# Layer 2's gate matmuls turned round: gate weights stationary in four column groups of TensorE

## The chip, the core and the metric

The kernel runs on one core of one Trainium2 chip. The metric is the device time of one execution in microseconds (us). The core has a matrix engine (TensorE, PE in the profile, with its weight loads shown as PEld), a vector engine (DVE), a scalar engine (ACT), GpSimd (POOL) and a queue engine that issues DMAs (SP). Each has its own queue of instructions and takes them in order.

## What is computed

Four graph layers follow each other on `x` [16, 1024, 128] with one adjacency matrix `adj` [16, 1024, 1024] of zeros and ones; after each of them stands a residual and a layer norm. The change lies in layer 2, whose gates are three columns per node:

```python
# layer 2 (L2_gnn); F = 128, ig_w, fg_w, og_w are [1, 256]
h = x @ W_w.T + W_b
e = (h @ A) @ h.T;  e = e + swap(e)
att = softmax(where(adj > 0, e, 0), axis=1) * adj
h_prime = relu(att @ h)
concat = concatenate([x, h_prime], axis=-1)          # [.., 256]
i_c = sigmoid(concat @ ig_w.T + ig_b)                # one number a node
f_c = sigmoid(concat @ fg_w.T + fg_b)
o_c = sigmoid(concat @ og_w.T + og_b)
h_joint = sigmoid(i_c * h_prime + f_c * x)
return o_c * tanh(h_joint)
# x = layernorm(x + layer 2);  layer 3 (two graph convolutions) follows
```

## The kernel before

The work is in three stretches: layer 0 with the loading of `adj` (up to about 750 us of the span), layer 1 with its sequential thinning of the adjacency (to about 1900 us), and layers 2 and 3 together (about 1930 us to the end, 3075 us). The change touches the last stretch.

There the 16 batches go through three generators, which `in_turn` lets take turns: for each `b`, `attention(b)` runs beside `after(b - 1)` and `before(b + 1)`. `before` makes layer 1's output (products of `hb` with `Wl`, turned into `yn`), adds it to `xn`, norms it (`normed`) and makes `xT`, `hT`, `G`, `hn`. `attention` has eight tiles of 128 nodes: two score matmuls (`pmm`, line 723), a masked maximum on DVE (`em`, L1564), an Exp on ACT (L1568), a scale by the sum (`hs`, L1575) and two matmuls into `acc` (L1578). `after` makes `hpT`, the relu of `acc` (L1584), the gates (L1585 to L1593), the gated sum `yn` (L1596 to L1603), a norm, and then layer 3: eight casts of the adjacency to `A` (four on ACT, L1614, four on DVE, L1627), `x3T` (L1618), a product with `U0` and two elu (L1490 to L1492 and L1486 to L1488), a product with `U1` (L1501) whose result is split into `zhi` and `zlo`, a propagation by `A` (L1515, 32 matmuls), the same again with `U2`, and the sum and its norm.

The gates before are 16 small matmuls a batch. For each tile `i` of 128 nodes, the nodes are the stationary operand and the three gate vectors stream past them:

```python
pg = ps_h.tile([P, NT, 3], F32, name="pg", tag="h")
for i in range(NT):
    c = slice(i * P, (i + 1) * P)
    nc.tensor.matmul(pg[:, i, :], s.xT[:, c], gw[:, 0, :], start=True, stop=False)
    nc.tensor.matmul(pg[:, i, :], hpT[:, c], gw[:, 1, :], start=False, stop=True)
```

The result `pg` has nodes on partitions, which is what the gating needs. It lives in the PSUM pool `ps_h`, which has two buffers, shared by every turned tile and every product of `before` and `after`. A float32 matmul with a full stationary operand shows as two weight loads and two matmul records in the trace; a transpose by `identf` shows as one of each.

`normed` takes eight BatchNorm statistics on DVE (L777, L779), a power on GpSimd (L744), a small product on DVE (`ln_nb`, L782) and eight ACT instructions on `xn` (L784).

The order of the instructions in each engine's queue is not that of the text: a scheduler sets it when the kernel is built, from its own estimate of durations and from which buffers are free. The generators only give it the sequence of the program.

Of the kernel before, what the change touches and what calls it, by code (L numbers as in the profile page):

```python
# [9 lines left out]
F32 = mybir.dt.float32  # L10
# [12 lines left out]
P = 128  # L23
# [616 lines left out]
def fast_kernel(ctx: ExitStack, tc: tile.TileContext, t: dict, out: bass.AP, flag: bass.AP):  # L640

    nc = tc.nc
    B, N, D = t["x"].shape
    NT = N // P
# [6 lines left out]
    identf = consts.tile([P, P], F32, name="identf")  # L651
# [34 lines left out]
    def nat(ap):  # L686
        return ap.rearrange("(t p) d -> p t d", p=P)

    def row_bcast(pool, src, n, name, bufs=1):

        v = pool.tile([P, n], F32, name=name, bufs=bufs)
        nc.sync.dma_start(v, bass.AP(tensor=src.tensor, offset=src.offset, ap=[[0, P], [1, n]]))
        return v

    def column(pool, src, name):
        v = pool.tile([P, 1], F32, name=name)
        nc.sync.dma_start(v, bass.AP(tensor=src.tensor, offset=src.offset, ap=[[1, P], [1, 1]]))
        return v

    def matrix(pool, src, name, bufs=1):  # L700
        v = pool.tile([P, P], F32, name=name, bufs=bufs)
        nc.sync.dma_start(v, src)
        return v

    def transposed(pool, psum, src, name, tag="tr"):
        v = pool.tile([P, P], F32, name=name)
        p = psum.tile([P, P], F32, name="wtr", tag=tag)
        nc.tensor.transpose(p, src, identf)
        nc.vector.tensor_copy(v, p)
        return v  # L710
# [16 lines left out]
    def tiles3(ap):  # L727
        return ap.rearrange("p (t d) -> p t d", d=P)

    def per_row(v):  # L730

        return v[:, :, None].to_broadcast([P, NT, P])
# [28 lines left out]
    def products(psum, *pairs):  # L761

        for p, c, _ in halves(psum):
            for i, (W, x) in enumerate(pairs):
                nc.tensor.matmul(p, W, x[:, c], start=(i == 0), stop=(i == len(pairs) - 1))  # L765
            yield p, c

    def half_rows(v):

        return v[:, :, None].to_broadcast([P, 4, P])  # L770
# [42 lines left out]
    def symmetric(pool, psum, A, name, tag="tr"):  # L813
        As = pool.tile([P, P], F32, name=name)
        p = psum.tile([P, P], F32, name="wtr", tag=tag)
        nc.tensor.transpose(p, A, identf)
        nc.vector.tensor_add(As, A, p)
        return As
# [49 lines left out]
    with ExitStack() as ph:  # L868

        early = ph.enter_context(tc.tile_pool(name="l0_early", bufs=1, reuse_waits="tile"))  # L870
        wts = ph.enter_context(tc.tile_pool(name="l0_w", bufs=1, reuse_waits="tile"))
        ps_w = ph.enter_context(tc.tile_pool(name="l0_pw", bufs=2, space=PSUM, reuse_waits="tile"))
        ps_a = ph.enter_context(tc.tile_pool(name="l0_pa", bufs=1, space=PSUM, reuse_waits="tile"))
        ps_h = ph.enter_context(tc.tile_pool(name="l0_ph", bufs=2, space=PSUM, reuse_waits="tile"))
# [7 lines left out]
        gw = wts.tile([P, 2], F32, name="l0gw")  # L882
        with nc.allow_non_contiguous_dma(reason="a vector of 256"):
            nc.sync.dma_start(gw, t["L0_gnn_gate_w"].rearrange("o (h d) -> d (o h)", d=P))
        gb = row_bcast(wts, t["L0_gnn_gate_b"], 1, "l0gb")
# [285 lines left out]
    class Layers23:  # L1171
# [8 lines left out]
        def weights(self, ps_h):  # L1180
            wts = self.wts
            self.Wl = wts.tile([P, 3, P], F32, name="Wl")
            nc.sync.dma_start(self.Wl, nat(t["L1_gnn_Wl"]))
            self.blcol = column(wts, t["L1_gnn_bl"], "blcol")
            self.W2T = transposed(wts, ps_h, matrix(wts, t["L2_gnn_W_w"], "l2W"), "l2WT", "h")
            self.b2 = column(wts, t["L2_gnn_W_b"], "l2b")
            self.As2 = symmetric(wts, ps_h, matrix(wts, t["L2_gnn_A"], "l2A"), "l2As", "h")
            self.gw = wts.tile([P, 2, 3], F32, name="l2gw")
            self.gb = wts.tile([P, 3], F32, name="l2gb")
            for i, n in enumerate(("ig", "fg", "og")):  # L1190
                with nc.allow_non_contiguous_dma(reason="a vector of 256"):
                    nc.sync.dma_start(self.gw[:, :, i], t[f"L2_gnn_{n}_w"].rearrange("o (h d) -> d (o h)", d=P))
                src = t[f"L2_gnn_{n}_b"]
                nc.sync.dma_start(self.gb[:, i:i + 1], bass.AP(tensor=src.tensor, offset=src.offset, ap=[[0, P], [1, 1]]))
            self.U = [matrix(wts, t[f"L3_gnn_W{i}"], f"U{i}") for i in range(3)]
            self.c = [column(wts, t[f"L3_gnn_b{i}"], f"c{i}") for i in range(3)]
            self.nbig = wts.tile([P, 1], F32, name="nbig")
            nc.vector.memset(self.nbig, -BIG)
# [26 lines left out]
    with ExitStack() as ph:  # L1225
        wts = ph.enter_context(tc.tile_pool(name="l1_w", bufs=1, reuse_waits="tile"))
# [5 lines left out]
        ps_h = ph.enter_context(tc.tile_pool(name="l1_ph", bufs=4, space=PSUM, reuse_waits="tile"))  # L1232
# [232 lines left out]
    with ExitStack() as ph:  # L1465
# [4 lines left out]
        ps_h = ph.enter_context(tc.tile_pool(name="l2_ph", bufs=2, space=PSUM, reuse_waits="tile"))  # L1470

        W2T, b2, As2, gw, gb, nbig, blcol, Wl = l2.W2T, l2.b2, l2.As2, l2.gw, l2.gb, l2.nbig, l2.blcol, l2.Wl
# [3 lines left out]
        def wide(name, bufs=1, dtype=F32):  # L1476
            return work.tile([P, N], dtype, name=name, bufs=bufs)

        def rows(name, bufs=1, dtype=F32):
            return work.tile([P, NT, P], dtype, name=name, bufs=bufs)  # L1480
# [100 lines left out]
        def after(s, b):  # L1581

            hpT = wide("hpT")
            nc.scalar.activation(hpT, s.acc, AF.Relu)  # L1584
            pg = ps_h.tile([P, NT, 3], F32, name="pg", tag="h")  # L1585
            for i in range(NT):
                c = slice(i * P, (i + 1) * P)
                nc.tensor.matmul(pg[:, i, :], s.xT[:, c], gw[:, 0, :], start=True, stop=False)
                nc.tensor.matmul(pg[:, i, :], hpT[:, c], gw[:, 1, :], start=False, stop=True)
            gt = small.tile([P, NT, 3], F32, name="gt")  # L1590
            nc.vector.tensor_add(gt, pg, gb[:, None, :].to_broadcast([P, NT, 3]))
            nc.scalar.activation(gt, gt, AF.Tanh, scale=0.5)
            nc.vector.tensor_scalar(gt, gt, 0.5, 0.5, op0=OP.mult, op1=OP.add)  # L1593
            yn = rows("yn", 2)
            for p, c, k in turned(ps_h, hpT):
                nc.vector.tensor_mul(yn[:, k, :], tiles3(p), half_rows(gt[:, k, 0]))  # L1596
            f = rows("x3T")
            nc.vector.tensor_mul(f, s.xn, per_row(gt[:, :, 1]))
            nc.vector.tensor_add(yn, yn, f)
            nc.scalar.activation(yn, yn, AF.Tanh, scale=0.5)  # L1600
            nc.scalar.activation(yn, yn, AF.Tanh, scale=0.5, bias=half)
            nc.vector.tensor_mul(yn, yn, per_row(gt[:, :, 2]))
            nc.vector.tensor_add(s.xn, s.xn, yn)  # L1603
            yield
            normed(small, s.xn)
            diag = bass.AP(tensor=s.A8.tensor, offset=s.A8.offset, ap=[list(s.A8.ap[0]), [N + P, NT], [1, P]])
            nc.vector.tensor_tensor(diag, diag, identb[:, None, :].to_broadcast([P, NT, P]), op=OP.add, saturate=False)
            dB = wide("dB")
            nc.sync.dma_start(dB, bass.AP(tensor=dinv_d.tensor, offset=dinv_d.offset + b * N, ap=[[0, P], [1, N]]))
            yield  # L1610

            A = work.tile([P, NT, N], F32R, name="A")
            for jt in range(NT // 2):
                nc.scalar.copy(A[:, jt, :], s.A8[:, jt, :])  # L1614
            db = dinv[:, b * NT:(b + 1) * NT]
            x3T = wide("x3T")
            for p, c, _ in turned(ps_h, s.xn):
                nc.scalar.copy(x3T[:, c], p)  # L1618
            h0 = wide("ehi", 2)
            for p, c in products(ps_h, (U0, x3T)):  # L1620
                elu(h0[:, c], p, c0)
            h1 = wide("ehi", 2)
            for h in range(H2):
                c = slice(h * 512, (h + 1) * 512)
                elu(h1[:, c], h0[:, c], None)
            for jt in range(NT // 2, NT):
                nc.vector.tensor_copy(A[:, jt, :], s.A8[:, jt, :])  # L1627
            yield
            parts = scaled_parts(h1, U1, db)
            yield  # L1630
            r = propagated(parts, A, dB)
            h2 = wide("ehi", 2)
            for h in range(H2):
                c = slice(h * 512, (h + 1) * 512)
                elu(h2[:, c], r[:, c], c1)
            yield
            parts = scaled_parts(h2, U2, db)
            yield
            r = propagated(parts, A, dB)
            nc.scalar.activation(r, r, AF.Identity, bias=c2)  # L1640
            yield
            for p, c, k in turned(ps_h, r):
                nc.vector.tensor_add(s.xn[:, k, :], s.xn[:, k, :], tiles3(p))
            normed(small, s.xn)
            nc.gpsimd.dma_start(nat(out[b]), s.xn)
            yield
# [49 lines left out]
```

## Time and profile before

| what | value |
|---|---|
| median of 15 runs | 3075.3 us (3066.54 to 3083.15) |
| the profiled execution | 3077.22 us, its span 3075.4 us |
| mean granted TensorE clock in it | 0.965 |
| PE / DVE / ACT / POOL busy | 93% / 76% / 66% / 10% |
| the chain that ended last, by engine | PE 61%, issue 17%, DVE 13%, ACT 4% |
| `pg` matmul records | 512, the first at 1934.6 us, the last at 3000.6 us |

The busy shares are over the whole span, and matmuls are pipelined, so that PE's busy time counts each record from its start to its modelled end. The granted clock is the share of TensorE's full speed that the throttle let through; the profile gives it for any stretch. Times within the span are read as us from its start; a period below is the time from the first gate matmul of one batch to that of the next.

### The profile page before, as it was taken

What the parts mean: (1) busy time and instruction counts of PE and PEld (TensorE: products, weight loads), DVE (VectorE), ACT (ScalarE), POOL (GpSimd) and SP (SyncE); (2) the same over time, 40 slices, a digit from 0 to 9 for tenths busy, and PEclk for the clock granted to TensorE, in tenths of its full rate; (3) what the DMA queues carried; (4) which work ended last, traced back from release to release, by engine and by line L of the source; (5) the groups of instructions that cost most, each with busy time, mean ns of one, the idle gap of its engine ahead of it and who ended that gap; (6) DMA issues with size and microseconds to landing.
All of it is one profiled execution on the core that took longest, in us unless ns stands there. A gap on an engine that the chain in (4) does not pass through costs nothing.

```text
span 3075.4 us, 43116 instructions
## 1 busy us (share of the span) xinstructions
PE 2856.3 (93%) x15379; PEld 1838.2 (60%) x15442; DVE 2327.9 (76%) x5971; ACT 2015.2 (66%) x3393; POOL 314.7 (10%) x292
## 2 busy tenths in 40 slices
PE   7999999997899999999999987999999999999995
PEld 4454555444566566777788874556555555555554
DVE  8788888886899996666688785766767676767765
ACT  6777777775678877565555534766666666667753
POOL 0000000003000001111122231000000000000000
PEclk9999999998999999999999998999999999999997
DMA  5344334441000014223367693111121221111000
GB/s 187 124 137 151 130 131 151 136 133 40 2 2 2 2 79 161 83 93 121 124 214 238 241 329 109 35 55 55 62 69 55 63 76 60 55 55 55 21 14 22
DMA packets 123216, 297.98 MB, mean 97 GB/s; under 512 B 12656, under 2 KB 64624, under 8 KB 115824
## 3 DMA queue, kind: packets, MB, share of 16 engines
q1 hardware_dynamic: 102384, 211.13, 20.7%
q0 software_dynamic: 20608, 84.00, 7.4%
q8 instruction: 124, 2.03, 0.3%
q14 instruction: 100, 0.82, 0.1%
HBM read 211.04 MB, written 84.02 MB: 96 GB/s over the span
## 4 chain that ended last, share of the span: by engine, by line
PE 61%; issue 17%; DVE 13%; ACT 4%; POOL 3%; DMA 2%; SPq 0%; POOLq 0%; DVEq 0%; ACTq 0%
PE pmm L723 10%; PE acc L1272 10%; PE ph L1515 7%; PE ph L765 6%; PE acc L1578 6%; PE acc L956 5%; PE ph L758 4%; PE ph L1376 4%; PE ph L1501 2%; POOL ln_rstd L744 2%; PE acc L1249 2%; ACT xn L784 2%; DVE ln_st L777 2%; DMA an<-in_adj 1%; DVE carry L908 1%
## 5 line engine op out<-in xcount | busy, mean ns | idle before, releaser
L723 PE MATMUL pmm<-G,hT 128*128 128x512 f32 x1024 | 522.1, 627 | 17.2 <-DVE mx L945 14.7
L723 PEld LDWEIGHTS pmm<-G,hT 128*128 128x128 f32 x1024 | 182.3, 198 | 182.4 <-issue 114.1
L1578 PE MATMUL acc<-em,hs 128*128 128x512 f32 x512 | 257.1, 614 | 12.1 <-DVE hs L1575 10.5
L956 PE MATMUL acc<-em,hs 128*128 128x512 f32 x512 | 240.5, 606 | 24.6 <-DVE hs L953 23.3
L784 ACT ACTIVATE xn<-xn,ln_nb,ln_rstd 128x128 f32<-128x128 f32 x512 | 206.5, 481 | 80.5 <-DVE ln_nb L782 80.4
L1272 PE MATMUL acc<-a,lo 128*128 128x512 f32 x768 | 241.1, 398 | 2.0 <-DVE lo L1240 2.0
L1272 PE MATMUL acc<-a,hi 128*128 128x512 f32 x768 | 241.8, 399 | 1.1 <-ACT hi L1239 0.9
L744 POOL TENSOR_TENSOR ln_rstd<-ln_rstd,mhalf 128x8 f32<-128x8 f32 x64 | 105.4, 1647 | 1297.6 <-DVE ln_rstd L741 1226.9
L1121 ACT ACTIVATE q<-s,negc 128x512 f16<-128x512 f32 x256 | 170.5, 697 | 59.4 <-DVE negc L1100 22.3
L1119 PE MATMUL s<-step,carry 128*128 128x384 bf16 (+3 forms) x1034 | 199.1, 303 | 7.9 <-DVE carry L1089 3.2
L1564 DVE CUSTOM_DVE_ANT_0 em<-pmm,msk 128x1024 f32<-128x1024 f32 x128 | 156.0, 1219 | 53.2 <-PE pmm L723 50.6
L1133 ACT ACTIVATE carry<-pc,negone 128x512 fp8e4<-128x512 f32 x256 | 166.8, 699 | 38.2 <-PE pc L1132 29.0
L900 ACT ACTIVATE ab<-an 128x1024 bf16<-128x1024 f32 x128 | 134.6, 1052 | 73.8 <-PE pt L907 36.5
L903 DVE SCALAR_TENSOR_TENSOR chk<-an 128x1024 fp8e4<-128x1024 f32 x128 | 156.2, 1220 | 35.0 <-DMA an<-in_adj 34.4
L956 PEld LDWEIGHTS acc<-em,hs 128*128 128x128 f32 x512 | 93.7, 191 | 143.1 <-issue 105.9
L1559 ACT ACTIVATE msk<-A,nbig 128x1024 bf16<-128x1024 fp8e4 x128 | 146.0, 1141 | 49.5 <-DVE mx L1564 47.6
L942 ACT ACTIVATE msk<-carry,l0nbig 128x1024 bf16<-128x1024 fp8e4 x128 | 145.4, 1140 | 44.5 <-DVE mx L945 40.4
L908 DVE TENSOR_SCALAR carry<-pt 128x1024 fp8e4<-128x1024 bf16 x128 | 155.8, 1219 | 23.4 <-PE pt L907 23.4
L1272 PEld LDWEIGHTS acc<-a,lo 128*128 128x128 f32 x768 | 142.8, 188 | 42.9 <-DVE lo L1240 9.5
L1272 PEld LDWEIGHTS acc<-a,hi 128*128 128x128 f32 x768 | 141.6, 188 | 34.0 <-ACT hi L1239 1.4
L945 DVE CUSTOM_DVE_ANT_0 em<-pmm,msk 128x1024 f32<-128x1024 f32 x128 | 155.4, 1214 | 6.9 <-PE acc L956 4.8
L949 ACT ACTIVATE em<-em,nmx 128x1024 f32<-128x1024 f32 x128 | 145.9, 1140 | 20.8 <-DVE nmx L947 17.3
(278 smaller groups left out, 6524.9 us busy)
## 6 DMA issues: line engine op xcount, KB each, us to landing
an<-in_adj SPq DMA_DIRECT2D x128, 512.0 KB, 3.3
adj_d<-carry POOLq DMA_DIRECT2D x16, 1024.0 KB, 4.9
A<-dil_d SPq DMA_DIRECT2D x16, 1024.0 KB, 6.7
rdeg<-rdeg_d SPq DMA_DIRECT2D x32, 512.0 KB, 4.2
ag_d<-ag POOLq DMA_DIRECT2D x32, 512.0 KB, 5.3
ag<-ag_d SPq DMA_DIRECT2D x32, 512.0 KB, 6.2
A<-adj_d SPq DMA_DIRECT2D x16, 1024.0 KB, 4.8
xn<-in_x SPq DMA_DIRECT2D x16, 512.0 KB, 3.9
```

Of the source, the lines that this page charges most:

```text
L723: nc.tensor.matmul(p[:, h * 512:(h + 1) * 512], lhsT, rhs[:, h * 512:(h + 1) * 512], start=True, stop=True)
L744: nc.gpsimd.tensor_tensor(r, r, mhalf[:, :n], op=OP.pow)
L765: nc.tensor.matmul(p, W, x[:, c], start=(i == 0), stop=(i == len(pairs) - 1))
L784: nc.scalar.activation(r[:, i, :], r[:, i, :], AF.Identity, scale=rstd[:, i:i + 1], bias=nb[:, i:i + 1])
L908: nc.vector.tensor_scalar(Y[b][:, :, it * P:(it + 1) * P], pt, 0.0, None, op0=OP.is_gt, saturate=False)
L956: nc.tensor.matmul(s.acc[:, c], hs, em[:, c], start=(jt == 0), stop=(jt == NT - 1))
L1119: nc.tensor.matmul(s[:, lo or 0:], y, twos if lo is None else step[:, :512 - lo], start=(j == 0), stop=(j == len(terms) - 1))
L1121: nc.scalar.activation(q[:, h * 512:(h + 1) * 512], s, AF.Abs, bias=st.negc[:, i:i + 1])
L1133: nc.scalar.activation(Y[b][:, hb, ks], pc, AF.Relu, bias=negone, saturate=False)
L1272: nc.tensor.matmul(acc, part[:, jt, :], pieces[h * NT // 2 + i][:, j, :], start=(jt == 0 and p == 0), stop=(jt == NT - 1 and p == 1))
L1515: nc.tensor.matmul(p, part[:, jt, :], A[:, jt, c], start=(jt == 0 and i == 0), stop=(jt == NT - 1 and i == 1))
L1578: nc.tensor.matmul(s.acc[:, c], hs, em[:, c], start=(jt == 0), stop=(jt == NT - 1))
```

## The change

The gate weights become the stationary operand, padded with zeros to 32 columns, and the nodes stream past them. The 1024 nodes are cut into four quarters of 256; each quarter goes to a column group of 32 columns of TensorE and lands on 32 partitions of one PSUM tile `pq`. The result has gates on partitions, so ACT copies it to SBUF (into the tile of `x3T`, which is free then) and two transposes bring nodes to partitions again. Beside that, the gate weights are zeroed once by DVE before their three DMAs fill in the real columns.

```diff
+    def gates(psum, out, *pairs):
+        p = psum.tile([P, N // 4], F32, name="pq", tag="h")
+        for i, (g, x) in enumerate(pairs):
+            for q in range(4):
+                nc.tensor.matmul(p[32 * q:32 * q + 32, :], g, x[:, q * N // 4:(q + 1) * N // 4], start=(i == 0),
+                                 stop=(i == len(pairs) - 1), tile_position=(0, 32 * q))
+        nc.scalar.copy(out, p)
+        p = psum.tile([P, 2, P], F32, name="pg", tag="h")
+        for t in range(2):
+            nc.tensor.transpose(p[:, t, :], out[:, t * P:(t + 1) * P], identf)
+        return p.rearrange("p t (q g) -> p q t g", q=4)
...
-            self.gw = wts.tile([P, 2, 3], F32, name="l2gw")
+            self.gw = wts.tile([P, 2, 32], F32, name="l2gw")
+            nc.vector.memset(self.gw, 0.0)
...
-            pg = ps_h.tile([P, NT, 3], F32, name="pg", tag="h")
-            for i in range(NT):
-                c = slice(i * P, (i + 1) * P)
-                nc.tensor.matmul(pg[:, i, :], s.xT[:, c], gw[:, 0, :], start=True, stop=False)
-                nc.tensor.matmul(pg[:, i, :], hpT[:, c], gw[:, 1, :], start=False, stop=True)
+            pg = gates(ps_h, wide("x3T")[:, :N // 4], (gw[:, 0, :], s.xT), (gw[:, 1, :], hpT))
             gt = small.tile([P, NT, 3], F32, name="gt")
-            nc.vector.tensor_add(gt, pg, gb[:, None, :].to_broadcast([P, NT, 3]))
+            nc.vector.tensor_add(gt.rearrange("p (q t) g -> p q t g", t=2), pg[:, :, :, :3],
+                                 gb[:, None, None, :].to_broadcast([P, 4, 2, 3]))
```

The diff is the whole edit, but since the scheduler sets the order of the queues, the orders of PE, DVE, ACT and SP differ from the first batch of layer 2 to the end. The orders of the changed program, as built, are known; its times are not.

## The prediction

> **What bounds the kernel now.** I read the page, then the stretches by batch, then layer 2's clock in steps of 1 us, then the tile `pg` and one batch's timeline by engine.
>
> ```profile
> span 3075.4 us, 43116 instructions
> PE 2856.3 (93%) x15379; PEld 1838.2 (60%) x15442; DVE 2327.9 (76%) x5971; ACT 2015.2 (66%) x3393; POOL 314.7 (10%) x292
> ```
>
> Two neighbouring periods (stretch and length, busy time of PE, PEld, DVE, ACT, POOL, granted clock) and two single microseconds after a gate burst:
>
> ```profile
> 2085.00:2157.00 72.00, 70.23 (x265) 42.50 (x264) 50.10 (x155) 47.76 (x94) 5.86 (x4) 0.95 0.18 59
> 2157.00:2227.40 70.40, 68.67 (x266) 41.29 (x265) 50.18 (x155) 48.10 (x94) 5.85 (x4) 0.98 0.18 60
> ...
> 2088.00:2089.00 1.00, 1.00 (x7) 1.00 (x6) 0.00 (x0) 0.00 (x0) 0.00 (x0) 0.50 0.69 221
> 2095.00:2096.00 1.00, 1.00 (x4) 0.49 (x3) 1.00 (x2) 1.00 (x4) 0.00 (x0) 1.00 0.00 0
> ```
>
> PE is empty for 1.7 us in a period, so layer 2 is PE's. The second thing is the clock. It comes in whole steps: each episode at half clock loses 1.7 or 3.4 us of PE, and from 2013 to 2950 us (13 periods, 937.4 us, 72.1 each) they add up to 42.6 us, 3.3 a period. At full clock a period would be 68.8. In the whole of layer 2, 14 episodes begin inside or just behind a gate burst and lose 32 us; most of the others come some 26 us later, where PE turns `xn` and waits for it.
>
> The burst itself:
>
> ```profile
> L1588 PE MATMUL pg<-l2gw,xT x256: 166/252/355, 1934.6 to 3000.3; 128*128 128x3 f32 x128
> L1589 PE MATMUL pg<-l2gw,hpT x256: 168/252/355, 1946.5 to 3000.6; 128*128 128x3 f32 x128
> L1591 DVE TENSOR_TENSOR gt<-pg,l2gb x16: 182/183/183, 1950.0 to 3000.9; 128x24 f32<-128x24 f32 x16
> ```
>
> That is 32 records a batch. They start 0.11 us apart (2157.10 to 2160.7), the pace of weight loads: 3.6 us a batch, 57 us in all.
>
> **What the change removes and adds on PE.** The 32 records go. In come 8 matmuls of 256 columns, by the two records of each float32 matmul 16 records, and two transposes. Score records of 512 columns start 0.43 us apart, so one of 256 takes 0.215. No row shows column groups. Four abreast give 4 x 0.215 = 0.9 us, one after another 16 x 0.215 = 3.4. I take a value between: the two records of one quarter need the same columns and stand next to each other in the queue, so only the second record of a quarter and the first of the next can overlap, 9 steps, 1.9 us. [...] The gate block is then 2.3 us (1.3 to 3.8), the transposes 2 x 0.11. PE saves 3.6 - 2.5 = 1.1 a batch (from 2.1 down to -0.4).
>
> [...]
>
> [...] The memset costs nothing: it stands beside the memset of `nbig`, which ran at 1774.0, and the DMAs into `l2gw` were issued from 1785.6. If it came late, SP's loads of `hT` and `ag` behind those DMAs would wait with them. On SP the load of `xn` moves ahead of those of `hb`; these are needed a period later. It costs nothing while the store of `xn` lands in time (a late one, 8 us, is on the chain once in before, around 2750 us).
>
> **The clock.** A burst of three-column matmuls hardly moves data through the array; 256-column ones do. I take the 32 us behind the bursts as gone (bounds 0 and 32).
>
> So far the change brings (1.1 + 2.0) x 16 = 50 us. The next part takes it back.
>
> **What the new order does.** The copy is a new link: PE's two transposes wait for ACT, and behind them in PE's queue stand the turning of `hpT` and all scores. ACT's copy stands behind two or three casts of `A`, which end 1.7 us after the block's start, so the wait is short; one half `pmm` covers it. The dear part is what moved behind it. Before, the gates' tanh came directly, and the norm's eight instructions after it (ACT, then DVE, then PE):
>
> ```profile
> 2160.99 0.22 ACT L1592 ACTIVATE gt<-gt 128x24 f32<-128x24 f32 x1 [2.16 <-DVE gt L1591]
> 2164.54 3.17 ACT L784 ACTIVATE xn<-xn,ln_nb,ln_rstd 128x128 f32<-128x128 f32 x8
> ...
> 2179.82 0.17 DVE L782 SCALAR_TENSOR_TENSOR ln_nb<-ln_mv,ln_rstd 128x8 f32<-128x8 f32 x1 [1.25 <-POOL ln_rstd L744]
> ...
> 2180.57 2.26 PE L758 MATMUL ph<-identf,xn 128*128 128x128 f32 x6 [0.64 <-ACT xn L784]
> ```
>
> In the new queues tanh stands behind those eight, which need `ln_nb`, which needs GpSimd's power (1.65 us). I walked PE, DVE, ACT and GpSimd through one period with these rows' durations, at full clock, from the first gate matmul (0; in before 2157.1). The order alternates between two forms; this is the one with two casts behind `hpT`, old times in brackets:
>
> - Gate block ends at 2.3, the half score at 3.2, its `em` (1.22) at 4.6, `ln_rstd` 4.8, GpSimd 6.6, `ln_nb` 6.7; the eight `xn` run 6.8 to 9.9; tanh at 10.0 (3.9).
> - `yn` by the gate 10.4 to 11.7 (6.5 to 7.7). PE meanwhile runs three scores; it loses 0.35 waiting for `em` and 0.5 at `hb`, whose PSUM buffer `yn` frees.
> - The two tanh of `yn` stand behind three Exps and a mask: second one done 17.8 (14.9). Product, sum, statistics, GpSimd: `ln_nb` 25.3 (22.7).
> - PE turns `xn` from 25.9, paced by ACT until 28; it was out of work at 25.1. It loses 2.1.
> - `U0` ends 31.7 (31.0). Behind it stand two `acc` and two `pmm` (3.4 us) where before one `acc` and five `pmm` stood (5.2). The elu, with the diagonal (1.22) and four `xn` now between its steps, ends 38.5 (35.8). PE is empty for 3.3.
> - `U1`, one `acc`, eight turns, two `acc`: the first propagation starts 43.9 (41.3).
> - From there to the next gates before took 29.0; one `acc` fewer makes it 28.1. Period 72.0.
>
> The other form, walked likewise: `ln_nb` 26.0, elu 36.9, propagation 40.7, then one `acc` more: 70.6. Mean 71.3. The unknown price of the block moves only the first form, by -1.0 to +1.4, because in the other DVE's statistics end later than the block: 70.8 to 72.0.
>
> So at full clock a period costs 71.3 against 68.8: PE has less to do, but stands empty for some 6 us instead of 1.7. Empty PE is what half clock follows here: before, two waits of 0.8 and 0.64 around the turning of `xn` were enough for an episode in about half of the periods. With 2 and 3.3 us empty I expect at least one of 1.7 a period; a second falls partly into the waits. I take 2.0 (0 to 3.4): period 73.3, 1.2 more than 72.1.
>
> **The sum.** 13 periods x 1.2 = +16 us. The last batch's chain loses the burst and gains block, copy and turns, about even; the first batch likewise. Profiled execution 3077.2 + 16 = 3093; it lies 1.9 above the median, so 3091.
>
> **Rivals.**
> 1. *PE's work decides throughout* (faster): if the waits that I walked are absorbed, because the elu and `yn` chains run closer than the queues say, PE's 1.1 and the clock's 2.0 a batch remain: 3075 - 50 = 3025; with four abreast 3010. For: PE 93% busy. Against: the order of ACT. It holds if `ln_nb` of `xn` comes no later than about 23 us into the period. Chance 0.13.
> 2. *The waits come, the clock stays up* (faster): the periods are 70.8 to 71.3, 13 x -0.8 to -1.3: 3058 to 3065. For: before's waits did not always bring an episode. Chance 0.15.
> 3. *The column groups don't run beside each other* (slower): 3.8 us of block, 72.0, and with both episodes 75.4: +3.3 x 13, 3118. For: no row shows groups beside each other. Chance 0.15.
> 4. *Even* (within 6 us): waits and clock cancel. Chance 0.09.
>
> The forecast has the remaining 0.48. About 0.2%, 6 us, is what a measurement of this kernel can tell from no change. Faster: 0.13 + 0.15 = 0.28; same 0.09; slower 0.63. The range reaches from between rivals 1 and 2 to just past rival 3: 3045 to 3122. The slower cases alone lie in 3082 to 3122.
>
> **What would show it.** Right: the second gates' `gt` tanh some 10 us behind the first `pq`; the `xn` turned at about 26 with a wait of 2 us for L784; a wait of 2 to 3 us of L1501 for DVE's `ehi`; PE's empty time near 6 us a period; clock near 0.97. The block: second records of one quarter and first of the next with the same start, 0.215 apart otherwise. No half clock right behind the block. Wrong if the periods are under 70, if L1501 does not wait, or if `pq` takes over 4 us.

## The result: 12.7 us faster, where 16 us slower was forecast

| | before | changed |
|---|---|---|
| median | 3075.32 us (50 runs, 3066.54 to 3083.67) | 3062.61 us (10 runs, 3055.19 to 3067.22) |
| ratio of the medians, 95% interval | | 0.9957 [0.9947, 0.9966] |
| profiled execution, span, mean clock | 3077.22, 3075.4 us, 0.965 | 3064.04, 3062.3 us, 0.971 |

Rival 2 had given 3058 to 3065 us. The head of the changed kernel's page and its chain line:

```profile
span 3062.3 us, 42692 instructions
PE 2808.5 (92%) x15155; PEld 1778.8 (58%) x15218; DVE 2335.6 (76%) x5972; ACT 2017.8 (66%) x3409; POOL 320.9 (10%) x292
...
PE 52%; DVE 20%; issue 17%; ACT 4%; POOL 4%; DMA 2%; SPq 0%; POOLq 0%; DVEq 0%; ACTq 0%
```

PE's busy time fell by 47.8 us, the span by 13.1. PE's share of the chain fell from 61% to 52%, and DVE's rose from 13% to 20%: PE now waits more for others. That is the outline of the answer: PE got back much more time than the whole program.

**The gate block.** The tile `pq` (durations min/median/max, first and last start), and PE's rows around one block (start, length):

```profile
L774 PEld LDWEIGHTS pq<-xT,l2gw x128: 105/108/110, 1939.1 to 2986.6; 128*32 128x32 f32 x128
L774 PE MATMUL pq<-xT,l2gw x128: 378/391/404, 1939.1 to 2986.8; 128*32 128x256 f32 x128
...
2087.05 1.02 PE L723 MATMUL pmm<-G,hT 128*128 128x512 f32 x2
2088.00 0.64 PE L774 MATMUL pq<-xT,l2gw 128*32 128x256 f32 x8
2088.46 0.62 PE L774 MATMUL pq<-hpT,l2gw 128*32 128x256 f32 x8
2089.00 1.13 PE L723 MATMUL pmm<-G,hT 128*128 128x512 f32 x2
```

Starts tell the cost. Eight records take 0.46 us, two rounds of four at 0.23, and the next score starts 1.00 us after the block began. The four records of a round start within 0.03 us of each other. So all four groups ran abreast. The two score records before the block took 0.95 us to give way, where their pace of 0.43 makes 0.86, and the second eight took 0.54 where the first took 0.46: going into and out of the groups cost 0.09 and 0.08 us.

**The order.** ACT's rows behind the same block:

```profile
2089.54 0.37 ACT L776 COPY x3T<-pq 128x256 f32<-128x256 f32 x1
...
2093.41 3.19 ACT L798 ACTIVATE xn<-xn,ln_nb,ln_rstd 128x128 f32<-128x128 f32 x8 [0.82 <-DVE ln_nb L796]
2096.51 0.20 ACT L1604 ACTIVATE gt<-gt 128x24 f32<-128x24 f32 x1
```

The tanh of the gates comes 8.5 us behind the block's start and behind the eight norm instructions, as foreseen. And PE's waits over the 13 periods (us in total, times, longest):

```profile
PE ph L1516 <- DVE ehi L1503: 23.7, 13, 2.6
PE ph L758 <- ACT xn L798: 16.9, 13, 2.2
```

These are the two waits of the prediction, in place. The periods alternate between the two forms that were walked. In the second form (from 2088.00) the waits take 1.63 us for `ehi` and 2.19 for `xn`; in the first (from 2300.74 and 2441.78) they take 1.54 to 2.60 and 0.53, where 3.3 and 2.1 had been walked.

**The periods.** Three of the changed kernel's (start:end, length, PE busy, then the other engines, clock), and single microseconds right behind a gate block:

```profile
2088.00:2158.61 70.61, 65.51 (x249) 37.71 (x249) 50.60 (x155) 48.30 (x95) 6.83 (x4) 0.98 0.17 60
2300.74:2371.03 70.29, 67.64 (x253) 38.32 (x253) 50.47 (x155) 48.05 (x95) 5.85 (x4) 0.98 0.18 60
2441.78:2511.76 69.98, 66.02 (x254) 37.56 (x253) 50.17 (x155) 48.14 (x95) 5.85 (x4) 1.00 0.17 61
...
2090.00:2091.00 1.00, 1.00 (x8) 0.86 (x8) 1.00 (x4) 0.00 (x0) 0.00 (x0) 1.00 0.42 82
2091.00:2092.00 1.00, 1.00 (x4) 0.40 (x3) 0.54 (x5) 0.65 (x1) 0.46 (x1) 1.00 0.75 246
```

I split every period of every kernel in the same way: what the clock took (sum over microseconds of 1 minus the granted clock), PE's empty time (length less PE busy), and the rest, PE's work as if at full clock. Means over the 13 steady periods, in us, for all kernels that follow:

| kernel | median | period | PE's work | lost to the clock | PE empty |
|---|---|---|---|---|---|
| before | 3075.3 | 72.11 | 67.03 | 3.28 | 1.80 |
| changed | 3062.6 | 70.89 | 65.12 | 1.71 | 4.06 |
| e1_full | 3069.1 | 70.88 | 67.36 | 0.00 | 3.52 |
| e2_wide | 3092.1 | 73.82 | 66.47 | 2.63 | 4.72 |
| e3_first | 3036.8 | 68.96 | 64.64 | 0.79 | 3.53 |
| e4_before_first | 3077.4 | 71.64 | 66.67 | 1.97 | 3.00 |
| e5_whole | 3044.6 | 68.96 | 64.63 | 0.92 | 3.41 |
| e6_tied | 3032.7 | 68.23 | 64.65 | 1.18 | 2.40 |
| e7_tied_full | 3083.4 | 71.95 | 67.64 | 0.92 | 3.39 |
| e8_before_late | 3082.8 | 71.90 | 67.58 | 2.10 | 2.22 |

For the change: work -1.91, clock -1.57, empty +2.26, together -1.22 a period and -15.9 over 13; the spans differ by 13.1. The first gate block came 4.5 us later than before (1939.07 against 1934.56); most of that difference, 4.25 us, stands already behind layer 0, at 788 us, where the two programs are the same, and it is one execution's against another's.

### The profile page after: what moved, and what is told of

Read it like the earlier page. It is cut to its first block, busy times and chain, and to the rows that moved or that the text cites. A ratio compares the mean times of both kernels' runs of the same rounds, so it can differ in the third digit from the quotient of the medians.

```text
span 3062.3 us, 42692 instructions
## 1 busy us (share of the span) xinstructions
PE 2808.5 (92%) x15155; PEld 1778.8 (58%) x15218; DVE 2335.6 (76%) x5972; ACT 2017.8 (66%) x3409; POOL 320.9 (10%) x292
## 4 chain that ended last, share of the span: by engine, by line
PE 52%; DVE 20%; issue 17%; ACT 4%; POOL 4%; DMA 2%; SPq 0%; POOLq 0%; DVEq 0%; ACTq 0%
PE acc L1287 10%; PE ph L1530 7%; PE pmm L723 6%; PE ph L765 5%; PE acc L970 5%; PE acc L1593 4%; PE ph L1391 4%; PE ph L758 3%; POOL ln_rstd L744 3%; DVE ln_st L791 3%; DVE em L1579 2%; PE ph L1516 2%; ACT xn L798 2%; PE acc L1264 2%; DMA an<-in_adj 1%
## 5 line engine op out<-in xcount | busy, mean ns | idle before, releaser
L723 PE MATMUL pmm<-G,hT 128*128 128x512 f32 x1024 | 510.8, 612 | 23.0 <-DVE mx L959 15.8
L723 PEld LDWEIGHTS pmm<-G,hT 128*128 128x128 f32 x1024 | 175.3, 193 | 183.5 <-issue 107.2
L744 POOL TENSOR_TENSOR ln_rstd<-ln_rstd,mhalf 128x8 f32<-128x8 f32 x64 | 112.1, 1752 | 1310.0 <-DVE nmx L1581 606.6
L1147 ACT ACTIVATE carry<-pc,negone 128x512 fp8e4<-128x512 f32 x256 | 166.5, 698 | 38.5 <-PE pc L1146 29.1
L914 ACT ACTIVATE ab<-an 128x1024 bf16<-128x1024 f32 x128 | 134.6, 1052 | 77.3 <-PE pt L921 36.9
L1579 DVE CUSTOM_DVE_ANT_0 em<-pmm,msk 128x1024 f32<-128x1024 f32 x128 | 155.7, 1217 | 26.8 <-PE acc L1593 22.1
L956 ACT ACTIVATE msk<-carry,l0nbig 128x1024 bf16<-128x1024 fp8e4 x128 | 145.5, 1140 | 45.9 <-DVE mx L959 40.9
```

Source lines behind the costliest of these rows:

```text
L723: nc.tensor.matmul(p[:, h * 512:(h + 1) * 512], lhsT, rhs[:, h * 512:(h + 1) * 512], start=True, stop=True)
L744: nc.gpsimd.tensor_tensor(r, r, mhalf[:, :n], op=OP.pow)
L1147: nc.scalar.activation(Y[b][:, hb, ks], pc, AF.Relu, bias=negone, saturate=False)
L1579: nc.vector.tensor_tensor_reduce(em, e, msk, 1.0, 0.0, op0=OP.add, op1=OP.max, accum_out=mx)
```

## The experiments

Three things could hold the gain or eat it: the block's own time on PE, the clock behind it, and the order, in which tanh stands behind the norm. The experiments change one of them at a time, as far as the scheduler lets them. The first four kernels ran beside before at 3076.4 us, the last four beside before at 3078.9.

**e1_full: the same block without column groups**

```diff
-                nc.tensor.matmul(p[32 * q:32 * q + 32, :], g, x[..quarter q..], ..., tile_position=(0, 32 * q))
+                nc.tensor.matmul(p, g, x[..quarter q..], start=(i == 0 and q == 0), stop=(i == len(pairs) - 1 and q == 3))
...
-            self.gw = wts.tile([P, 2, 32], F32, name="l2gw")
+            self.gw = wts.tile([P, 2, P], F32, name="l2gw")
```

> The changed kernel without column groups: the gate weights are padded to 128 columns, the eight matmuls of a batch fill the whole array and all add into one 128x256 tile (three quarters of the gates are left out and the rest is a sum over quarters, so the gate values are not the reference's); copy and turns stay. Theory (the block's length counts only in part, the periods are set by the chain of the gates through ACT and DVE): 16 records at 0.215 us make the block 3.4 to 3.6 us instead of 1.0, the period grows by 1 to 2 us, 3062 becomes 3075 to 3090. Rival (PE's work decides): + 2.5 us in each of 16 batches, 3102. Rival (the block is hidden): 3062. The order of the queues differs a little from the changed kernel's, so 5 us either way say nothing.

Measured: 3069.06 us, 0.9981 of before [0.9967, 0.9994], 6.5 us over the changed kernel.

```profile
2228.40 1.89 PE L774 MATMUL pq<-xT,l2gw 128*128 128x256 f32 x8
2230.13 1.89 PE L774 MATMUL pq<-hpT,l2gw 128*128 128x256 f32 x8
2231.85 2.74 PE L723 MATMUL pmm<-G,hT 128*128 128x512 f32 x6
...
2228.40:2299.07 70.67, 67.17 (x251) 39.73 (x250) 51.02 (x155) 48.42 (x95) 5.85 (x4) 1.00 0.17 60
```

All quarters add up in the same rows here. The block takes 3.45 us (2228.40 to 2231.85), 16 x 0.215, so the groups are worth 2.45 us of PE a batch, a ratio of 3.45. Yet the period is the same to 0.01 us: 2.24 more work, 1.71 less lost clock (not one episode in 13 periods) and 0.54 less empty time. The 6.5 us stand mostly in the last stretch, from the second last gates to the last ones: 54.0 us against 47.2, with 5.1 us of lost clock in it against 1.7. The median lies between the theory's 3075 to 3090 and the 3062 of the second rival, that the block is hidden. In this run, the column groups bring nothing to a steady period.

**e2_wide: the old form, with 64 gate columns instead of three**

```diff
-            self.gw = wts.tile([P, 2, 3], F32, name="l2gw")
+            self.gw = wts.tile([P, 2, 64], F32, name="l2gw")
+            nc.vector.memset(self.gw, 0.0)
...
-            pg = ps_h.tile([P, NT, 3], F32, name="pg", tag="h")
+            pg = ps_h.tile([P, NT, 64], F32, name="pg", tag="h")
...
-            nc.vector.tensor_add(gt, pg, gb[:, None, :].to_broadcast([P, NT, 3]))
+            nc.vector.tensor_add(gt, pg[:, :, :3], gb[:, None, :].to_broadcast([P, NT, 3]))
```

> The kernel before with the gate vectors padded to 64 columns, so that each small matmul streams 64 columns instead of 3; nothing else. Theory (half clock behind the burst comes from matmuls that stream next to nothing): the pace of 0.11 us a record stays, the episodes at half clock within 4 us of the bursts (27 us from the second batch's gates to the fifteenth's) go, those at the turning of xn stay or grow to one a period; 3075 becomes 3050 to 3060. Rival (the clock falls for weight loads, whatever streams): 3075 within 6. If the records slow to over 0.13 us, the burst grows by more than 0.6 us a batch, + 10 us in all.

Measured: 3092.11 us, 1.0059 [1.0039, 1.0080], far above the theory's 3050 to 3060. The scheduler answered with another order, and the periods alternate between two lengths. In the long ones tanh stands behind the eight norm instructions and one gate matmul runs 12 us ahead of the other fifteen; in the short ones tanh stands in front and the burst is whole. Two periods, and the start of the first of them on PE:

```profile
2300.55:2378.20 77.65, 70.82 (x265) 42.96 (x264) 51.26 (x160) 49.87 (x98) 5.85 (x4) 0.93 0.16 55
2378.20:2447.31 69.11, 66.98 (x265) 40.12 (x264) 48.87 (x151) 46.38 (x90) 5.85 (x4) 1.00 0.18 61
```

```profile
2300.55 0.33 PE L1589 MATMUL pg<-l2gw,xT 128*128 128x64 f32 x2
...
2303.74 4.54 PE L723 MATMUL pmm<-G,hT 128*128 128x512 f32 x6 [1.95 <-DVE mx L1565]
```

Half clock begins 4 us into six of the seven long periods, but that is behind the one early matmul and this wait of 1.95 us. Behind the fifteen matmuls that follow at 2312.28, and behind the whole bursts of the six short periods, there is none: 0 of 13, where before it was 11 of 13. The records start 0.11 us apart as before. So the episodes behind the bursts went as the theory expected, which speaks for the three columns as the source and against the weight loads of the rival: these took 0.192 us each (median) with three columns and with 64. The order changed as well. The run also shows what order can do: two periods with the same number of PE records (265) differ by 8.5 us, 4.7 of it empty PE (6.83 and 2.13) and 5.1 lost clock, while PE's work is 1.3 smaller in the longer one.

**e3_first: the changed kernel with the norm behind the next gates**

The last norm and the store of a batch are recorded after the gates of the next batch, so that tanh need not stand behind them. As written here, the norm and store of batch 14 are left out, in this kernel and in e4_before_first.

```diff
+            if tails:
+                tails.pop()()          # behind the sigmoid of gt
...
-            normed(small, s.xn)
-            nc.gpsimd.dma_start(nat(out[b]), s.xn)
+            def tail():
+                normed(small, s.xn)
+                nc.gpsimd.dma_start(nat(out[b]), s.xn)
+            if b == B - 1:
+                tail()
+            else:
+                tails.append(tail)
...
+        tails = []
```

> The changed kernel with the last norm and the store of a batch put behind the next batch's gates in the program, so that ACT has the gates' tanh ahead of the eight instructions on xn; same work. Theory (the waits of the changed kernel come from tanh behind the norm): tanh some 4 us after the first gate matmul instead of 8.5 to 9, the turning of xn at 23 to 24 us instead of 24.4 to 27, PE's empty time down from 4.2 to about 2.5 us a period, period 69 to 70 instead of 70.9: 3040 to 3053. Rival (PE's work and the clock set the period, the order of ACT does not): 3062 within 6.

Measured: 3036.83 us, 0.9879 [0.9860, 0.9898]; periods 68.96 instead of 70.89, 25 us over 13. The order costs the changed kernel about as much as the theory said, a little more. It did not come by the waits alone: PE's empty time fell by 0.53 a period, to 3.53 and not to the expected 2.5; 0.92 is lost clock and 0.48 PE's work.

**e4_before_first: the same move in the kernel before**

The diff of e3_first, on before.

> The kernel before with the same move as in the run before it. Here the scheduler makes the opposite of it: in the queue of ACT the gates' tanh comes behind five of the eight instructions on xn, where in the kernel before it came ahead of all. Same work, old gate matmuls. Theory (order sets the waits): the chain of the gates is 2 us later, PE's empty time grows from 1.7 to 3 or more us a period: 3080 to 3100. Rival (PE's work and the clock set the period): 3075 within 6.

Measured: 3077.41 us, 1.0006 [0.9994, 1.0019]. The scheduler put tanh behind five of the eight norm instructions in every other batch. As expected PE stood empty longer (3.00 instead of 1.80), but the clock lost less (1.97 instead of 3.28), and the periods came out 0.5 shorter; the last stretch gave that back (53.5 instead of 46.8). The expected loss did not come, and the time is the rival's. As in e1_full, there is more waiting and less lost clock; what ties the two together this run does not show.

**e5_whole: e3_first with nothing left out**

The diff is against e3_first.

```diff
-            if b == B - 1:
-                tail()
-            else:
-                tails.append(tail)
+            tails.append(tail)
+            if b == B - 1:
+                for f in tails:
+                    f()
```

> The changed kernel with the last norm and store of a batch recorded behind the next batch's gates (as e3_first, but with no batch's norm or store left out). Theory, that the gain of e3_first came from the gates' tanh no longer standing behind eight norm instructions: 3036 to 3045 us, periods 68.7 to 69.2 as there, and only the norm and store of batch 14 come on top, in the last stretch (0 to 5 us). Rival, that e3_first was fast because that norm and store were left out: its periods were 68.96 each over 13 batches that left nothing out, so no more than the last stretch can change; if the rival holds it is 3050 us or more.

Measured: 3044.61 us, 0.9891 [0.9877, 0.9905]; periods 68.96 as in e3_first. So it was not the norm and store left out that made e3_first fast: the rival falls. ACT's order is now the intended one:

```profile
2163.66 0.21 ACT L1604 ACTIVATE gt<-gt 128x24 f32<-128x24 f32 x1
2164.66 3.18 ACT L798 ACTIVATE xn<-xn,ln_nb,ln_rstd 128x128 f32<-128x128 f32 x8 [0.80 <-DVE ln_nb L796]
```

This kernel shows something else as well. Two neighbouring periods, the first with one half-clock episode, the second with none:

```profile
2159.08:2227.78 68.70, 66.02 (x251) 37.72 (x250) 50.27 (x155) 48.08 (x95) 5.99 (x4) 0.98 0.18 62
2227.78:2296.55 68.77, 64.55 (x251) 36.97 (x250) 50.27 (x155) 48.04 (x95) 6.08 (x4) 1.00 0.19 62
...
2183.00:2184.00 1.00, 1.00 (x4) 0.49 (x3) 1.00 (x4) 1.00 (x4) 0.00 (x0) 0.50 0.00 0
2252.00:2253.00 1.00, 1.00 (x6) 0.63 (x5) 1.00 (x5) 1.00 (x4) 0.00 (x0) 1.00 0.00 0
```

The episode begins 22.6 us into the period and loses 1.70 us, and the period is not longer. PE's empty time is 2.68 with it (68.70 - 66.02) and 4.22 without (68.77 - 64.55). The queues of PE, DVE and ACT hold the same instructions in the same order in both. Behind the episode eight score records run through; without it PE stands still in the middle of the same eight:

```profile
2189.47 3.77 PE L723 MATMUL pmm<-G,hT 128*128 128x512 f32 x8
...
2260.06 1.98 PE L723 MATMUL pmm<-G,hT 128*128 128x512 f32 x4 [1.66 <-DVE mx L1579]
```

All 13 periods are of these two kinds, seven with an episode and six without, and all but the last, which holds more instructions, take 68.6 to 69.0. **The 1.70 us of clock that were lost ahead of this wait were eaten by it**: DVE came no later for them. Where little waiting follows, most of it is paid: e6_tied, below, has periods of 67.0 to 67.3 us without an episode and 68.0 to 68.5 with one (the last period, and one with 3.41 us lost, left aside).

**e6_tied and e7_tied_full: form against form, with the norm tied behind tanh**

In both, the norm is recorded late as in e5_whole, and a copy of a gate into the norm's bias tile forces it behind tanh; e7_tied_full also has the two edits of e1_full. The part that differs from e5_whole:

```diff
         nb = small.tile([P, NT], F32, name="ln_nb")
+        if behind is not None:
+            nc.vector.tensor_copy(nb, behind)       # behind = gt[:, :, 0]
...
```

> As e5_whole, but the norm's bias tile is first written from the gates (one small copy on DVE per batch), so that the norm can stand only behind the gates' tanh whatever the scheduler's costs say. It is there as the partner of e7_tied_full. The copy costs DVE about 0.2 us a batch (the like-sized bias step took 0.17). Theory: 3036 to 3050 us. If the norm, now late, becomes the wait that ends last at the second half's transposes, periods rise to 70 to 71 and it is 3055 to 3065.

> As e6_tied, but without column groups: the gate weights are padded to 128 columns, and all eight matmuls go one after the other over the whole array into one 128x256 tile, so the gates' values are not the reference's. The block took 3.4 us instead of 1.0 in e1_full, and there it cost the period nothing. Theory A, that PE's work decides once the gates' tanh is in front: 2.4 us in each of 13 to 15 periods, 31 to 36 us over e6_tied, 3070 to 3085. Theory B, that the block costs its time but keeps the clock at full speed as in e1_full (0.00 lost, against 0.79 per period in e3_first): 20 to 25 us over e6_tied, 3057 to 3072. Theory C, that waits hide the block here as well: within 8 us of e6_tied.

Measured: e6_tied 3032.73 us, 0.9850 [0.9833, 0.9866], the fastest version of all and 3 us below its expected range; e7_tied_full 3083.43 us, 1.0021 [1.0010, 1.0032]. Windows, the first of e6_tied, the others of e7_tied_full:

```profile
2152.63:2219.70 67.07, 64.68 (x251) 37.09 (x251) 50.79 (x156) 48.36 (x95) 5.85 (x4) 1.00 0.19 63
```

```profile
2231.40:2306.23 74.83, 69.85 (x252) 40.52 (x250) 52.44 (x160) 49.96 (x99) 6.23 (x4) 0.98 0.17 57
2306.23:2374.97 68.74, 66.99 (x252) 39.74 (x251) 49.15 (x152) 46.54 (x91) 5.85 (x4) 1.00 0.18 62
...
PE ph L1518 <- DVE ehi L1505: 15.8, 6, 3.0
```

In the undisturbed periods, 67.07 against 68.74, the full array costs 2.31 more work and 0.64 less empty time: 1.67 us net. In these periods the groups do pay: theory C of the expectation falls, and A has the right kind, at about two thirds of its price. The median of e7_tied_full lies in A's range, but the 51 us between the two medians are more than any of the three theories gave. The rest is the other kind of period, 74.83 with 4.98 us empty, in which the scheduler's order makes PE wait for `ehi` up to 3.0 us. Longer gates change the scheduler's order too, so this pair compares form and order together.

**e8_before_late: the old form with the norm late and tanh first**

As e5_whole's edit on before, with the norm recorded after the first gated product, which keeps tanh ahead of the eight norm instructions on ACT in every batch.

```diff
             for p, c, k in turned(ps_h, hpT):
                 nc.vector.tensor_mul(yn[:, k, :], tiles3(p), half_rows(gt[:, k, 0]))
+            if tails:
+                tails.pop()()
```

> The kernel before (three-column gates), with the last norm and store of a batch recorded behind the next batch's gates and first products, nothing left out. ScalarE's order is that of before, with tanh ahead of the eight norm instructions; on DVE the norm's statistics come later. Theory, that before had little wait to lose (PE empty 1.7 us per period) and its excess is gate records and lost clock, so that the new form is needed for the gain: 3062 to 3080 us, clock lost 2 us or more per period. Rival, that the late norm is by itself what made e3_first and e5_whole fast: 3036 to 3055.

Measured: 3082.82 us, 1.0016 [1.0001, 1.0030], 3 us past the upper end of the theory's range and far from the rival's. A period with two episodes, one with none, and microseconds behind a gate burst of the first:

```profile
2159.08:2231.36 72.28, 70.57 (x266) 42.58 (x265) 49.82 (x155) 47.73 (x94) 5.85 (x4) 0.95 0.17 59
2303.59:2373.89 70.30, 67.39 (x265) 40.29 (x264) 49.91 (x155) 47.72 (x94) 5.85 (x4) 1.00 0.18 60
2162.00:2163.00 1.00, 1.00 (x7) 1.00 (x7) 0.00 (x0) 0.00 (x0) 0.00 (x0) 0.50 0.48 180
```

The late norm does not help the old form. Half clock follows 11 of its 13 bursts, 2 to 4 us into the period. Against e5_whole: work +2.95, clock +1.18, empty -1.19, together 2.94 a period; 13 times that is 38.2, and so are the medians apart (3082.82 - 3044.61). With the norm late on both sides, this is what the new form brings, together with the order that the scheduler gave each.

## Why the prediction was wrong

The sign was wrong; the mechanism that was to make it slower is there. Step by step:

- **The gate block, 2.3 us: too long.** The pairs theory failed; it is 1.00, past the low end of 1.3, and all four quarters start together. Its four rounds take 0.92 us, near the 0.9 that four abreast were to give. The 0.35 that stands beside the pairs' 1.9 in the 2.3, and in both ends of its range, was my allowance for going into and out of the block. No run shows that term; in its place the changed kernel shows 0.09 and 0.08 us. The prediction's own working says what the error is worth: 1.3 us in one of the two forms, hence -0.65 a period.
- **Half clock right behind the bursts gone, 32 us: right.** There is no half clock in the first 20 us of any of the 13 periods, in the changed kernel or in any other with the gate weights stationary (e1, e3, e5, e6, e7). (Outside these periods it begins once, 4.3 us behind e5_whole's last block, after three waits of PE.) The old form has it behind 11 of 13 bursts in before, in e4_before_first and in e8_before_late, three orders. That ties it to the form and not to the order, and e2_wide, with none behind 13 bursts of 64 columns, to the three columns. Why three-column matmuls bring it about no run shows.
- **Tanh behind the eight norm instructions: right**, at 8.6 to 8.9 us in the form that was walked to 10.0; the block's 1.3 is the difference.
- **The walk: too long in one form, right with luck in the other.** The second form was walked to 26.0, 36.9 and 40.7 for `ln_nb`, elu and propagation, period 70.6; in the batch from 2088.00 `ln_nb` comes at 26.3, `U1` starts at 37.4, the propagation at 40.9, and the period is 70.61, with 1.70 of lost clock in it that the walk did not have. That fit is partly luck. In all six periods of this form the power ahead of `ln_nb` took 2.62 us, where the walk had 1.65; at the walk's price `ln_nb` would have come at 25.4, 0.6 before the walk. The first form was walked to 25.9, 38.5 and 43.9 for the turning of `xn`, elu and propagation, period 72.0. In the batch from 2441.78, which had full clock throughout, they are 24.7, 36.6 and 41.7, period 69.98. Of these 2.0, the block is 1.3; some 0.7 remain that were walked too long. PE's empty time was to be near 6 us and is 4.06. The power from 2088.00:

```profile
2111.67 2.62 POOL L744 TENSOR_TENSOR ln_rstd<-ln_rstd,mhalf 128x8 f32<-128x8 f32 x1 [13.84 <-DVE sm L1586]
```

- **The clock's surcharge, 2.0 on top: the step that turned the sign.** 1.71 us a period was indeed lost, where the prediction had it, 26 to 36 us into the period. But the whole of it was added to waits that it can shorten. The changed kernel's `U1` in three periods of the first form, with a late episode (from 2158.61), with an early one (from 2300.74) and without (from 2441.78):

```profile
2194.91 3.41 PE L1516 MATMUL ph<-U,ehi 128*128 128x128 f32 x16 [2.60 <-DVE ehi L1503]
2337.68 2.05 PE L1516 MATMUL ph<-U,ehi 128*128 128x128 f32 x16 [1.54 <-DVE ehi L1503]
2478.38 2.05 PE L1516 MATMUL ph<-U,ehi 128*128 128x128 f32 x16 [2.59 <-DVE ehi L1503]
```

In the period from 2300.74 the episode begins 26.8 us in, ahead of the wait. The wait for `ehi` is 1.05 shorter than without an episode, `U1` starts at 36.94 instead of 36.60, and the period is longer by only 0.31 (70.29 and 69.98). (The period without an episode waits 0.26 near its start, which the others do not; without that, some 0.6 of the 1.71 would show.) Four of the seven periods of this form are like that. In two, the episode begins at 35.7 to 36.0 and slows `U1` itself, behind a wait of full length: these periods take 71.01 and 71.13, longer by 1.03 and 1.15.

In the second form the waits do not shrink. `U1` starts 3.94 or 3.95 us behind the start of the last record of `U0` in all six periods, and waits 1.63 or 1.64: what delays `U0` delays `ehi` too. The period with two episodes takes 72.05, the five with one 70.61 to 71.15.

In before, the empty time is 1.73 to 1.77 in 12 of 13 periods whatever the clock did, and the period is longer by 1.7 for each 1.7 lost (70.28 us with 1.7 lost, 72.05 with 3.4, 73.62 with 5.1). I had read the price of an episode from there and carried it into a kernel that waits. The prediction said that a second episode "falls partly into the waits"; in the first form, the first did too. Its reason for the episodes is not borne out either: empty PE alone does not bring them. e1_full stands empty for 3.5 us a period, about twice as long as in before, with waits of up to 1.2 us, and has none in 13 periods.

The sum again: 73.3 was forecast and 70.89 measured, 2.4 less. The first form, forecast at 74.0 with its surcharge, took 70.72 in the mean of seven: the block is 1.3 of the difference, the walk 0.7, and the surcharge 1.3, since some 0.7 of its 2.0 shows. The second, forecast at 72.6, took 71.10 in the mean of six; these 1.5 are surcharge and walk together, and the runs do not split them, since no period of this form ran at full clock. Without the surcharge the prediction's own period of 71.3 would have given faster even with the block at 2.3; that was rival 2, at 0.15. Its time came out, but not its condition: the clock did not stay up, 1.71 us a period were lost. Rival 1 (PE's work decides) needed the waits gone, and e5_whole and e6_tied, which put tanh ahead of the norm again, reach 3045 and 3033, on the way to its 3025. Rival 3 (groups one after another) is refuted by the block, and its price too: e1_full, a block of 3.45 us, is 3069 and not 3118.

What stays open: what an episode costs in the second form; why a period of e1_full, with more work than the changed kernel and less waiting, has no half clock at all, and so whether the groups' gain there is lost to the clock by cause or by the accident of its order; and how much of e7_tied_full's loss is the block's own.

## What to carry to other kernels

A change of an instruction's form is also a change of every queue's order when a scheduler sets it: here PE's work shrank by 1.9 us a batch, the new order took 2.3 us in waits, and recording the norm later (e5_whole, e6_tied) gave 18 to 30 us on top of the change, by the medians. Lost clock and waits were not simply added up in these runs. In e5_whole a slow stretch that lost 1.70 us ahead of a wait for DVE did not lengthen the period (68.70 us with it, 68.77 without). In the changed kernel's second form what delayed `U0` delayed DVE's `ehi` too: `U1` started 3.94 or 3.95 us behind the start of the last record of `U0` in all six periods. And in before, where PE was empty for 1.73 to 1.77 us in 12 of 13 periods whatever the clock did, each 1.7 us lost made the period 1.7 longer (70.28, 72.05 and 73.62 us with 1.7, 3.4 and 5.1 lost). When a walk through the queues ends in waits, price the clock inside the walk: run PE's instructions more slowly there (the 16 records of `U1` took 3.41 us with an episode on them, 2.05 without) and see if the waiting instruction comes later.

## What the runs showed of the hardware

- Four column groups of 32 columns, with float32 records of 256 columns, ran at 0.23 us per round of four in the changed kernel, against 0.215 us for one record over the whole array in e1_full. The form's weight loads are shorter as well: 0.108 us (median) for 128x32 in the changed kernel against 0.190 for 128x128 in e1_full.
- Half clock followed 33 of 39 bursts of three-column float32 matmuls, in three kernels with three orders (11 of 13 each in before, e4_before_first and e8_before_late), and none of 13 with 64 columns at the same 0.11 us a record (e2_wide).
- TensorE's half clock came in steps that lose 1.71 us: in the changed kernel the granted clock was 0.50 from 2115.88 to 2119.29 us, 3.41 us, and 1.00 in the microsecond before and in the one after. What starts a step no run shows: the longest wait of PE in the changed kernel's steady periods is 2.6 us, and the episodes behind the three-column bursts come while the records show PE 100% busy.
- GpSimd's power on 128x8 elements took 1.64 to 1.66 us in most cases in the changed kernel, and 2.62 once in each of the six steady periods of the second form. What made it longer was not tried.
